# Even and odd fields on the two halves of the TensorE array, with 4-bank PSUM tiles, in a pairwise bilinear product

## Chip, cores, metric

One core of a Trainium2 chip. The metric is device time in microseconds (us) of one execution on that core. The kernel before takes 1359.69 us (median of 3 runs, 1359.48 to 1359.76). On one core a single run has no state of its own ("unknown"); where several runs were taken, all of them were fast.

## The reference

4096 rows, each with 32 fields of 64 numbers, and a 64 x 64 matrix W for each of the 496 pairs i < j of fields. All in float32; 520 MB are written.

```python
idx_i, idx_j = np.triu_indices(32, k=1)
vi = inputs[:, idx_i, :]                       # (4096, 496, 64)
vj = inputs[:, idx_j, :]
return jnp.einsum('bpd,pde->bpe', vi, W) * vj  # (4096, 496, 64)
```

## The kernel before

A row tile is 128 of the 4096 rows; there are 32. For each, TensorE multiplies x_i (turned, so that the 64 numbers of a field lie on partitions) with W for up to 16 pairs at once, into a PSUM tile. VectorE multiplies the PSUM tile with x_j into an output tile; five output tiles (groups of pairs) leave per row tile. The contraction is only 64 long: in the trace these matmuls take 64 rows of the array (`64*128`), the transposes 128 (`128*128`). The kernel uses both halves of the rows for the **same** pairs: half 0 makes the first 32 of the 64 output columns, half 1 the others.

```python
E2 = D // 2                 # 32
CH = BANK // E2             # 16 pairs a step
...
psum = ctx.enter_context(tc.tile_pool(name="psum", bufs=4, space=bass.MemoryType.PSUM))
...
def order_w(c, k, copy):    # W put in order by a copy, in pieces
    ...
    copy(rp[:r], src[:, k * EU : (k + 1) * EU])
def turn_w(c, k, rp, copy): # then turned by TensorE
    ...
# a step: m <= 16 pairs of field i
ps = psum.tile([P, 2, CH, E2], F32, tag="ps", name=f"ps_{s}")   # 2 banks, four such tiles
...
for h in range(2):
    nc.tensor.matmul(ps[:, h, ...], xT[...][h * D : (h + 1) * D, ...], wT[c][h * D : (h + 1) * D, ...], ...)
...
if i in aside and c0 == 0:            # 7 steps of 46
    nc.scalar.copy(tmp, src)
    nc.gpsimd.tensor_mul(dst, tmp, xj)
else:
    nc.vector.tensor_mul(dst, src, xj)
```

For field i to be on either half, x is turned twice, in 32 transposes of neighbouring fields (0,1), (1,2), ..., eight to a PSUM tile. W is loaded in four transfers of 128 or 112 partitions.

Of the kernel before, what the change touches and what calls it, by code (L numbers as in the profile page):

```python
# [8 lines left out]
F32 = mybir.dt.float32  # L9


@with_exitstack
def kernel(
    ctx: ExitStack,
    tc: tile.TileContext,
    x: bass.AP,
    w: bass.AP,
    out: bass.AP,
):










    nc = tc.nc  # L30

    B, F, D = x.shape
    P = 128
    NB = 2
    assert 2 * D == P and B % (NB * P) == 0
    NBLK = B // (NB * P)
    NP = F * (F - 1) // 2
    E2 = D // 2
    BANK = 512
    CH = BANK // E2  # L40
    RUN = 2 * BANK // P
    p0 = [i * (F - 1) - i * (i - 1) // 2 for i in range(F)]


    groups = [(0, 3), (3, 7), (7, 11), (11, 17), (17, F - 1)]
    cap = max(p0[b] - p0[a] for a, b in groups)

    aside = (1, 3, 5, 7, 9, 11, 13)

    cuts = [*range(0, NP, P), NP]  # L50
    wrows = list(zip(cuts[:-1], cuts[1:]))

    const = ctx.enter_context(tc.tile_pool(name="const", bufs=1))
    xpool = ctx.enter_context(tc.tile_pool(name="xpool", bufs=2))
    xtpool = ctx.enter_context(tc.tile_pool(name="xtpool", bufs=4))
    tpool = ctx.enter_context(tc.tile_pool(name="tpool", bufs=3))
    opool = ctx.enter_context(tc.tile_pool(name="opool", bufs=3))
    psum = ctx.enter_context(tc.tile_pool(name="psum", bufs=4, space=bass.MemoryType.PSUM))

    ident = const.tile([P, P], F32, tag="ident", name="ident")  # L60
    make_identity(nc, ident)

    xs = {}

    def rows_of(dram: bass.AP, blk: int) -> bass.AP:
        return dram[blk * NB * P : (blk + 1) * NB * P]

    def new_x(blk: int):

        xs[blk] = xpool.tile([P, 1 + NB * F, D], F32, tag="xs", name=f"xs_{blk}")  # L70
        nc.gpsimd.memset(xs[blk][:, 0, :], 0.0)  # L71

    def load_x(blk: int, eng, k0: int = 0, k1: int = NB):
        src = rows_of(x, blk).rearrange("(p k) f d -> p (k f) d", k=NB)
        eng.dma_start(out=xs[blk][:, 1 + k0 * F : 1 + k1 * F, :], in_=src[:, k0 * F : k1 * F, :])


    wflat = w.rearrange("p d e -> p (d e)")
    raw, wT = {}, {}
    EU = 2 * BANK // P  # L80
    NU = E2 // EU

    def load_w(c: int):

        a, b = wrows[c]
        pool, tag = ((opool, "ot"), (xpool, "xs"), (const, "w3"), (xpool, "xs"))[c]
        raw[c] = pool.tile([P, D * D], F32, tag=tag, name=f"raw_{c}")
        nc.sync.dma_start(out=raw[c][: b - a, :], in_=wflat[a:b])

    def order_w(c: int, k: int, copy):  # L90
        r = wrows[c][1] - wrows[c][0]
        rp = tpool.tile([P, EU, 2, D], F32, tag="tmp", name=f"rp_{c}_{k}")
        src = raw[c][:r, :].rearrange("p (d h e) -> p e h d", h=2, d=D)
        copy(rp[:r], src[:, k * EU : (k + 1) * EU])  # L94
        return rp

    def turn_w(c: int, k: int, rp, copy):
        r = wrows[c][1] - wrows[c][0]
        if c not in wT:
            wT[c] = const.tile([P, r, E2], F32, tag=f"w{c}", name=f"wT_{c}")  # L100
        pt = psum.tile([P, EU, P], F32, tag="ps", name=f"ptw_{c}_{k}")
        for n in range(EU):
            nc.tensor.transpose(  # L103
                pt[:, n, :r], rp[:r, n].rearrange("p h d -> p (h d)"), ident[:r, :r]
            )
        copy(wT[c][:, :, k * EU : (k + 1) * EU], pt[:, :, :r].rearrange("p e r -> p r e"))  # L106

    def turn_x(blk: int, k: int, q: int, copy):

        pt = psum.tile([P, RUN, P], F32, tag="ps", name=f"ptx_{blk}_{k}_{q}")  # L110
        for n in range(RUN):
            s = k * F + q * RUN + n
            nc.tensor.transpose(  # L113
                pt[:, n, :], xs[blk][:, s : s + 2, :].rearrange("p f d -> p (f d)"), ident
            )
        xT = xtpool.tile([P, RUN, P], F32, tag="xT", name=f"xT_{blk}_{k}_{q}")
        copy(xT, pt)  # L117
        return xT


    steps = [
        (g, i, c0, min(CH, F - 1 - i - c0))
        for g, (a, b) in enumerate(groups)
        for i in range(a, b)
        for c0 in range(0, F - 1 - i, CH)
    ]
    NS = len(steps)
    first = {}
    for s, (_, i, _, _) in enumerate(steps):
        first.setdefault(i, s)  # L130


    AHEAD = 4
    due: dict = {}
    for t in range(NBLK * NB):
        for q in range(F // RUN):
            at = t * NS + (first[q * RUN - 1] if q else 0) - AHEAD
            due.setdefault(max(0, at), []).append(("x", t // NB, t % NB, q))
    for c, at in enumerate([None, (2, 4, 5, 7), (9, 11, 13, 15), (20, 22, 25, 28)]):
        for k in range(NU) if c else ():  # L140
            due.setdefault(at[k], []).append(("w", c, k))
    LATE = 6

    new_x(0)
    load_x(0, nc.scalar, 0, 1)
    load_w(0)
    load_w(1)
    load_x(0, nc.sync, 1, NB)
    load_w(2)

    v, p, a = nc.vector.tensor_copy, nc.gpsimd.tensor_copy, nc.scalar.copy
    xT = {(0, 0, 0): turn_x(0, 0, 0, v)}
    due[0] = [d for d in due[0] if d != ("x", 0, 0, 0)]
    rps = [order_w(0, k, copy) for k, copy in ((0, v), (1, p))]
    turn_w(0, 0, rps[0], a)
    rps.append(order_w(0, 2, v))
    turn_w(0, 1, rps[1], a)
    rps.append(order_w(0, 3, v))
    turn_w(0, 2, rps[2], v)
    turn_w(0, 3, rps[3], a)  # L160

    ot = None
    for s in range(NBLK * NB * NS):
        t, st = divmod(s, NS)
        blk, kt = divmod(t, NB)
        g, i, c0, m = steps[st]
        if st == LATE and kt == 0 and blk and blk + 1 < NBLK:
            new_x(blk + 1)
            load_x(blk + 1, nc.scalar)
        for what, *args in due.get(s, ()):  # L170
            if what == "x":
                xT[tuple(args)] = turn_x(*args, a)
            else:
                c, k = args
                turn_w(c, k, order_w(c, k, (v, p)[k % 2]), a)
                if k == NU - 1 and c == 1:
                    load_w(3)
                if k == NU - 1 and c == 3:
                    new_x(1)
                    load_x(1, nc.scalar)  # L180

        base, end = p0[groups[g][0]], p0[groups[g][1]]
        pa = p0[i] + c0
        if pa == base:
            ot = opool.tile([P, cap, D], F32, tag="ot", name=f"ot_{t}_{g}")
        ps = psum.tile([P, 2, CH, E2], F32, tag="ps", name=f"ps_{s}")
        for c, (lo, hi) in enumerate(wrows):
            lo, hi = max(pa, lo), min(pa + m, hi)
            if lo < hi:
                for h in range(2):  # L190
                    n = i + 1 - h
                    nc.tensor.matmul(  # L192
                        ps[:, h, lo - pa : hi - pa, :],
                        xT[blk, kt, n // RUN][h * D : (h + 1) * D, n % RUN, :],
                        wT[c][h * D : (h + 1) * D, lo - wrows[c][0] : hi - wrows[c][0], :],
                        start=True,
                        stop=True,
                    )
        o = pa - base
        j = 1 + kt * F + i + 1 + c0  # L200
        dst = ot[:, o : o + m, :].rearrange("p m (h e) -> p m h e", h=2)
        src = ps[:, :, :m, :].rearrange("p h m e -> p m h e")
        xj = xs[blk][:, j : j + m, :].rearrange("p m (h e) -> p m h e", h=2)
        if i in aside and c0 == 0:
            tmp = tpool.tile([P, CH, 2, E2], F32, tag="tmp", name=f"tmp_{s}")
            nc.scalar.copy(tmp, src)  # L206
            nc.gpsimd.tensor_mul(dst, tmp, xj)  # L207
        else:
            nc.vector.tensor_mul(dst, src, xj)  # L209
        if pa + m == end:  # L210
            nc.sync.dma_start(  # L211
                out=rows_of(out, blk).rearrange("(p k) n d -> p k n d", k=NB)[:, kt, base:end, :],
                in_=ot[:, : end - base, :],
            )
# [27 lines left out]
```

## Time and profile before

| | before |
|---|---|
| median, us | 1359.69 |
| span of the profiled run, us | 1357.5 |
| first output issued, us | 30.0 |
| row tile 0 complete (its fifth output issued), us | 71.6 |
| last output issued, us | 1342.1 |
| so a row tile takes, us | (1342.1 - 71.6) / 31 = 40.98 |

The last four rows come from the times at which the SP queue issued the output transfers. They split any span into a **head** (to the filling of tile 0), 31 times a **pace**, and a tail; all comparisons below use this split. The profile's lines for this kernel are in the prediction: the transfers run at 401 to 433 GB/s in all but the first two and the last slice, and they are the bound.

### The profile page before, as it was taken

The numbers are of one execution on the slowest core, as the hardware profiler recorded it, in microseconds if no ns is written. First come the engines' busy times: TensorE is split into PE (matmuls) and PEld (weight loads), VectorE is DVE, ScalarE is ACT, GpSimd is POOL, SyncE is SP. The second block draws the span as 40 slices with busy tenths as digits, with TensorE's granted clock in tenths as the row PEclk, the third lists the DMA queues.
The fourth block names the chain that finished last, engine by engine and source line by source line (L and its number), as shares of the span: only waits on it lengthen the run. The fifth ranks groups of instructions, "written<-read, shape, count | busy, mean of one in ns | idle before, by whom it ended". The sixth has DMA issues, their size and how long they took to land.

```text
span 1357.5 us, 17867 instructions
## 1 busy us (share of the span) xinstructions
PE 1171.5 (86%) x7424; PEld 681.2 (50%) x7424; DVE 951.3 (70%) x1259; ACT 371.1 (27%) x367; POOL 546.2 (40%) x253
## 2 busy tenths in 40 slices
PE   5998988888888888988889888899888889888894
PEld 4554554545455454554545445455454545545552
DVE  5686876767677676766667767677776777767783
ACT  3432322222222222222322222222222322223220
POOL 4544433443333443334434334433344433444441
PEclk9998998989999999998989999999898999999997
DMA  7999999999999999999999999999999999999997
GB/s 291 388 430 431 426 424 431 431 422 426 401 424 413 430 423 412 428 409 431 410 417 425 413 433 407 421 423 410 428 412 424 426 409 424 406 431 428 417 419 335
DMA packets 26128, 562.92 MB, mean 415 GB/s; under 512 B 2896, under 2 KB 2896, under 8 KB 2896
## 3 DMA queue, kind: packets, MB, share of 16 engines
q1 hardware_dynamic: 23744, 529.28, 92.0%
q10 hardware_dynamic: 2304, 32.51, 5.7%
q8 instruction: 58, 0.95, 0.3%
q14 instruction: 22, 0.18, 0.0%
HBM read 41.68 MB, written 520.09 MB: 414 GB/s over the span
## 4 chain that ended last, share of the span: by engine, by line
DMA 50%; PE 23%; DVE 18%; POOL 4%; issue 3%; ACT 0%; DVEq 0%; SPq 0%; POOLq 0%; ACTq 0%
DMA out_dram<-ot 49%; PE ps L192 19%; DVE ot L209 18%; PE ptx L113 4%; POOL ot L207 3%; DMA raw<-in_L_rec_W_dram 1%; POOL rp L94 1%; PE ptw L103 0%; ACT tmp L206 0%; DVE rp L94 0%; DVEq L209 0%; DVE xT L117 0%; ACT wT L106 0%; SPq L211 0%; POOLq L207 0%
## 5 line engine op out<-in xcount | busy, mean ns | idle before, releaser
L209 DVE TENSOR_TENSOR ot<-ps,xs 128x1024 f32<-128x1024 f32 (+15 forms) x1248 | 938.6, 807 | 378.4 <-DMA out_dram<-ot 195.3
L192 PE MATMUL ps<-wT,xT 64*128 64x512 f32 (+14 forms) x6272 | 1025.2, 467 | 118.0 <-DVE ot L209 105.5
L192 PEld LDWEIGHTS ps<-wT,xT 64*128 64x128 f32 x6272 | 554.0, 193 | 554.6 <-DVE ot L209 281.9
L207 POOL TENSOR_TENSOR ot<-tmp,xs 128x1024 f32<-128x1024 f32 x224 | 527.3, 2360 | 623.5 <-ACT tmp L206 397.7
L206 ACT COPY tmp<-ps 128x1024 f32<-128x1024 f32 x224 | 226.7, 1012 | 465.5 <-PE ps L192 460.6
L117 ACT COPY xT<-ptx 128x1024 f32<-128x1024 f32 x127 | 128.5, 1012 | 470.2 <-PE ptx L113 470.2
L113 PE MATMUL ptx<-ident,xs 128*128 128x128 f32 x1024 | 143.8, 285 | 48.9 <-DVE ot L209 34.3
L113 PEld LDWEIGHTS ptx<-ident,xs 128*128 128x128 f32 x1024 | 113.2, 144 | 95.4 <-issue 51.3
L71 POOL MEMSET xs<- 128x64 f32 x16 | 2.4, 151 | 146.7 <-DVE ot L209 146.7
L94 POOL COPY rp<-raw 128x1024 f32<-128x1024 f32 (+1 forms) x7 | 16.1, 2299 | 16.1 <-DMA raw<-in_L_rec_W_dram 11.8
L106 ACT COPY wT<-ptw 128x1024 f32<-128x1024 f32 (+1 forms) x15 | 14.7, 984 | 28.1 <-PE ptw L103 28.1
L103 PE MATMUL ptw<-ident,rp 128*128 128x128 f32 (+1 forms) x128 | 17.0, 280 | 3.2 <-DVE rp L94 2.0
L94 DVE COPY rp<-raw 128x1024 f32<-128x1024 f32 (+1 forms) x9 | 11.0, 1233 | 12.3 <-DMA raw<-in_L_rec_W_dram 11.9
L103 PEld LDWEIGHTS ptw<-ident,rp 128*128 128x128 f32 (+1 forms) x128 | 14.1, 145 | 10.2 <-issue 5.6
L106 ACT ACT_TABLE_LOAD x1 | 1.3, 1283 | 1.2 <-PEq L229 1.2
L117 DVE COPY xT<-ptx 128x1024 f32<-128x1024 f32 x1 | 1.2, 1208 | 0.0
L106 DVE COPY wT<-ptw 128x1024 f32<-128x1024 f32 x1 | 1.2, 1208 | 0.0
masks.py:197 POOL MEMSET ident<- 128x128 f32 x1 | 0.2, 205 | 0.3 <-POOLq L229 0.3
masks.py:199 POOL TENSOR_SCALAR_AFFINE_SELECT ident<-ident 128x128 f32<-128x128 f32 x1 | 0.3, 292 | 0.0
L229 POOL MEMSET const-float32-0.0<- 128x1 f32 x1 | 0.1, 98 | 0.2 <-issue 0.2
L229 POOL MEMSET const-bfloat16-1.0<- 128x1 bf16 x1 | 0.1, 101 | 0.0
L229 POOL MEMSET const-uint8-127<- 128x1 uint8 x1 | 0.1, 101 | 0.0
(1 smaller groups left out, 0.1 us busy)
## 6 DMA issues: line engine op xcount, KB each, us to landing
out_dram<-ot SPq DMA_DIRECT2D x64, 3360.0 KB, 16.2
out_dram<-ot SPq DMA_DIRECT2D x64, 2880.0 KB, 16.7
out_dram<-ot SPq DMA_DIRECT2D x32, 3392.0 KB, 17.2
xs<-in_r_inputs_dram ACTq DMA_DIRECT2D x15, 2048.0 KB, 16.6
raw<-in_L_rec_W_dram SPq DMA_DIRECT2D x3, 2048.0 KB, 15.6
raw<-in_L_rec_W_dram SPq DMA_DIRECT2D x1, 1792.0 KB, 15.7
xs<-in_r_inputs_dram ACTq DMA_DIRECT2D x1, 1024.0 KB, 11.4
xs<-in_r_inputs_dram SPq DMA_DIRECT2D x1, 1024.0 KB, 17.7
```

Of the source, the lines that this page charges most:

```text
L71: nc.gpsimd.memset(xs[blk][:, 0, :], 0.0)
L94: copy(rp[:r], src[:, k * EU : (k + 1) * EU])
L103: nc.tensor.transpose(pt[:, n, :r], rp[:r, n].rearrange("p h d -> p (h d)"), ident[:r, :r])
L106: copy(wT[c][:, :, k * EU : (k + 1) * EU], pt[:, :, :r].rearrange("p e r -> p r e"))
L113: nc.tensor.transpose(pt[:, n, :], xs[blk][:, s : s + 2, :].rearrange("p f d -> p (f d)"), ident)
L117: copy(xT, pt)
L192: nc.tensor.matmul(ps[:, h, lo - pa : hi - pa, :], xT[blk, kt, n // RUN][h * D : (h + 1) * D, n % RUN, :], wT[c][h * D : (h + 1) * D, lo - ...
L206: nc.scalar.copy(tmp, src)
L207: nc.gpsimd.tensor_mul(dst, tmp, xj)
L209: nc.vector.tensor_mul(dst, src, xj)
L229: nc = _bacc.Bacc("TRN2", target_bir_lowering=False, num_devices=1)
```

## The change

The intent: put **different** fields on the halves, even ones on half 0 and odd ones on half 1. All 64 columns of a pair then come from one half, so a matmul has 8 pairs x 64 columns, x needs 16 transposes, not 32, and W needs no ordering before it is turned. To have fewer and longer instructions, a PSUM tile holds 2 fields x 16 pairs, 4 banks (a bank is the program's `BANK`, 512 float32 numbers a partition); four tiles of 2 banks become two of 4.

```diff
-    E2 = D // 2
-    CH = BANK // E2
+    BP = BANK // D
+    PSB = 4
+    CH = PSB // 2 * BP
...
-    psum = ctx.enter_context(tc.tile_pool(name="psum", bufs=4, space=bass.MemoryType.PSUM))
+    psum = ctx.enter_context(tc.tile_pool(name="psum", bufs=2, space=bass.MemoryType.PSUM))
...
-        nc.sync.dma_start(out=raw[c][: b - a, :], in_=wflat[a:b])
+            while a < b:
+                n = min(16, b - a)
+                c = a - row0[f]
+                dst = (raw if a < P else wT[1])[a % P : a % P + n].rearrange(
+                    "r (h d) e -> r h (d e)", h=2
+                )
...
+                    nc.sync.dma_start(out=dst, in_=src)     # 26 loads in all, of 16 rows or fewer
...
-    def order_w(c: int, k: int, copy):
...
+    def turn_w(lo: int, hi: int, e0: int, copies):
+        src = (wT[1] if c else raw)[a : a + n].rearrange("r m e -> r e m")   # strided read
...
-        ps = psum.tile([P, 2, CH, E2], F32, tag="ps", name=f"ps_{s}")
+        ps = psum.tile([P, 2, CH, D], F32, tag="ps", name=f"ps_{s}")
+        for b0 in range(0, m, BP):
+            for h in range(halves):
+                nc.tensor.matmul(
+                    ps[:, h, b0:b1, :],
+                    xT[t][h * D : (h + 1) * D, f, :],
+                    wT[r // P][h * D : (h + 1) * D, r % P : r % P + b1 - b0, :],
...
-        if i in aside and c0 == 0:
+        if (f, c0) in aside and t:                # two steps of 24
+            nc.scalar.copy(dst, src)
+            nc.gpsimd.tensor_mul(dst, dst, xj)
```

W's row for field pair f holds the matrices of an even and an odd field side by side. Field pair f has 31 - 2f rows, in steps of up to 16: 16 + 15, 16 + 13, ..., 16 + 1, then single steps.

Passages are cut from the recorded prediction, each cut marked: what it took over, without a trace that shows it, on transfers, on PSUM and on the clock; when W was to be in, with rival D that went with it; and the reason that rival C gave for a falling clock. The sum stands as it was forecast, 1360 + 8 + 31 x 0.5 = 1383, put at 1380. The cut passage on when W is in belonged to the working behind the 8 us of the head; how much of the 8 came from it is not on record. The 0.05 us for a signal is the author's estimate (the trace has 0.06 from a multiply's end to the next weight load), and so is the 0.5 us added for the mesh.

> **What bounds the kernel now.** I read the page first, then the trace in four places: what the transfer queue waited for, the chain of waits, windows of the head, and windows of stretches in which VectorE never stops. The page's rates, queues and rows:
>
> ```profile
> PE 1171.5 (86%) x7424; PEld 681.2 (50%) x7424; DVE 951.3 (70%) x1259; ACT 371.1 (27%) x367; POOL 546.2 (40%) x253
> ...
> DMA  7999999999999999999999999999999999999997
> GB/s 291 388 430 431 426 424 431 431 422 426 401 424 413 430 423 412 428 409 431 410 417 425 413 433 407 421 423 410 428 412 424 426 409 424 406 431 428 417 419 335
> ...
> q1 hardware_dynamic: 23744, 529.28, 92.0%
> q10 hardware_dynamic: 2304, 32.51, 5.7%
> ...
> L209 DVE TENSOR_TENSOR ot<-ps,xs 128x1024 f32<-128x1024 f32 (+15 forms) x1248 | 938.6, 807 | 378.4 <-DMA out_dram<-ot 195.3
> L206 ACT COPY tmp<-ps 128x1024 f32<-128x1024 f32 x224 | 226.7, 1012 | 465.5 <-PE ps L192 460.6
> L113 PE MATMUL ptx<-ident,xs 128*128 128x128 f32 x1024 | 143.8, 285 | 48.9 <-DVE ot L209 34.3
> ```
>
> The two queues take 97.7% of the span, no slice is above 433 GB/s, and VectorE's largest wait is for an output transfer to free its tile. The kernel is bound by writing 520 MB. At 430 GB/s its 562.9 MB need 1309 us; the span is 1357.5. So whatever the change does for the engines, some 48 us is all there is to win. The chain of waits gives the pace:
>
> ```profile
> 369.57 20.33 DMA out_dram<-ot
> ...
> 452.17 20.34 DMA out_dram<-ot
> ```
>
> The same wait comes back after 82.6 us, two row tiles: 41.3 us a tile. A tile moves 17.3 MB (16.25 out, half of a 2.1 MB load of x), 40.2 us at 430 GB/s. So about 1 us a tile is lost now, and the rest of the 48 us lies in the head and the tail:
>
> ```profile
> 22.00:32.00 10.00, 10.00 (x62) 5.90 (x64) 7.19 (x8) 6.02 (x6) 5.40 (x3) 1.00 0.21 88
> ```
>
> (window, length, busy time of PE, weight load, VectorE, ScalarE and GpSimd, granted clock, transfer share, GB/s.) For some 8 us the queue has nothing to write while W is ordered and turned.
>
> **Where the small figures come from.** By shape, the multiply takes 1219 ns at 1024 elements and 219 ns at 64: 1.042 ns per element plus 0.15 us. Neighbouring multiplies overlap by 0.08 us (one starts at 594.20 and lasts 1.09, the next starts at 595.21). TensorE's pace:
>
> ```profile
> 604.41 0.19 PEld L192 LDWEIGHTS ps<-wT,xT 64*128 64x128 f32 x2 [0.24 <-issue]
> 604.84 0.19 PEld L192 LDWEIGHTS ps<-wT,xT 64*128 64x128 f32 x2 [0.23 <-issue]
> 605.11 1.01 ACT L206 COPY tmp<-ps 128x1024 f32<-128x1024 f32 x1 [3.02 <-PE ps L192]
> ```
>
> A pair of 512-column matmuls, one on each half of the array, follows the last after 0.43 us, and its reader starts 0.70 us after its weight load: 0.43 plus 0.27 (I take 0.30). From a multiply's end to the next weight load it is 0.06. Eight transposes are busy 1.09 us.
>
> [...] after 123.0 to 127.0 with 0.10 us of TensorE work, the clock is 0.54 in the next 7 us.
>
> **The change part by part.**
> *Matmuls.* 196 a tile become 79; the columns stay nearly the same (W's 256 rows of 64 columns on each half against 496 of 32). Array time goes to about 14 us a tile, and 16 transposes (2.2 us) replace 32 (4.4). All off the bound.
> *VectorE.* Of 24 steps a tile 22 stay on it. Both halves of a step have equal length, so 15 surplus pairs are multiplied and overwritten: 511 x 64 = 32,704 elements, less 2 x 2048 that ScalarE and GpSimd take, 28,608. 28,608 x 1.042 = 29.8, plus 22 x 0.07 = 1.5: 31.3 us (29.3 now, 938.6/32).
> *PSUM.* Four tiles of 2 banks become two of 4. TensorE can refill a tile only while the one multiply of the other runs. A refill takes 0.06 + 0.43 + 0.43 + 0.30 = 1.22 us. After a multiply of c rows on both halves (0.15 + 0.133c) VectorE stands idle for 1.38 less that (the 0.16 are two lost overlaps): c = 9, 7, 5, 3, 1 give 0.03, 0.30, 0.56, 0.83, 1.05, together 2.8 us a tile. Each of the two steps for ScalarE (0.16 + 0.833 x 2.048 = 1.87 us) holds one of the two tiles: 1.4 and 1.1 of idle, 0.2 after: 2.7. The turn of x holds one for 2.2 + 2.0 (two copies of 1.01): 2.0 us of idle before row 3 and 1.7 before the last: 3.7. Sum 9.2.
> *Surplus pairs again.* The built program makes ten multiplies a tile wait on VectorE itself, because each overwrites a surplus pair of the one before. Some six aren't hidden behind TensorE: 6 x 0.13 (0.08 overlap, 0.05 signal) = 0.8.
> Filling a tile thus takes 31.3 + 9.2 + 0.8 = 41.3 us, against 40.2 for its transfers. Two nearly equal stages with three output tiles between them don't mesh fully; I add 0.5: 41.8, against 41.3 now.
> *Head.* No ordering, but 26 loads of W go in, [...] Walked through with the durations above: first half of W at 11.7, its 64 transposes and copies to 21.4, first multiply 22.7, first output 38 (30.0 now), then four more turns of W interleaved with steps, group 1 at 50, tile 0 filled at 78 and written at 88. Before, 19.8 MB had moved by 60 us and 28.5 were needed, so tile 0 was written at about 80: 8 us worse.
> Sum: 1360 + 8 + 31 x 0.5 = 1383; with a slightly better mesh 1370. I say **1380**.
>
> **The rivals.** (A) As above: the two-tile exchange between TensorE and VectorE paces the kernel at about the transfers' speed: 1365 to 1400. (B) Transfers stay the only bound and the 1 us a tile that is lost now comes back, since there are fewer long stops of TensorE and so fewer slow refills: 1360 + 8 - 31 x 0.7 = 1346. For it: the queue is 97.7% busy now, and before's fill, with about 30 us of VectorE a tile, has slack. Against: the change takes that slack away. (C) The clock falls [...]; pairs at 0.86 would make a tile 48 us, the kernel 1540. Against it is this stretch, in which VectorE never stops and TensorE's columns fill under 40% of the time, at full clock:
>
> ```profile
> 679.00:681.00 2.00, 2.00 (x18) 1.20 (x14) 2.00 (x4) 0.29 (x1) 0.00 (x0) 1.00 1.01 426
> 681.00:683.00 2.00, 1.85 (x14) 0.90 (x12) 2.00 (x5) 0.00 (x0) 0.00 (x0) 1.00 0.99 426
> ```
>
> [...]
>
> **Range and chances.** Each 0.3 us a tile is 9 us, and my gaps are good to about 0.8 us a tile: 1350 to 1412. Faster by 2% means under 1332.5, below what even B reaches: 0.05. Slower by 2% starts at 1386.9, just above my centre: 0.40. Within 2%: 0.55.
>
> **What would show it.** Right: VectorE's busy time up to 970 to 1010 us; its waits for TensorE up from 157 to some 250 us or more, those for output transfers down from 195; the longest waits for TensorE ahead of the two small rows at a tile's end; the transfer share below 9 in many slices; the first output at 35 us or later. Wrong: flat 425 to 430 GB/s with VectorE waiting mainly for transfers (B, and the time below 1350), or a granted clock under 0.8 (C). I'd be wrong in size if a multiply of 2048 elements took something other than 2.29 us, or if refills took much less than 1.2.

## The result

The changed kernel takes **1752.38 us** (median of 4 fast runs, 1746.95 to 1756.72), the kernel before 1359.72 in the same rounds (4 fast runs, 1359.48 to 1364.54). The ratio is 1.2875, with a 95% interval of 1.2829 to 1.2921. Ratios in this document are the mean time of one kernel's fast runs over the mean of the other's fast runs of the same rounds, so not quite the ratio of the medians. The result is exact enough to pass against the reference. The time is far outside the predicted range of 1350 to 1412.

| us | before | after | difference |
|---|---|---|---|
| first output issued | 30.0 | 95.9 | |
| tile 0 complete (head) | 71.6 | 162.6 | +91.0 |
| 31 tiles | 31 x 40.98 | 31 x 50.94 | +308.7 |
| last output issued to the end (tail) | 15.4 | 9.3 | -6.1 |
| span | 1357.5 | 1751.1 | +393.6 |

So four fifths of the loss is the steady pace, one fifth the head. The page of the kernel after; its rows of groups give busy time and mean ns of one, then idle time of that engine just before them and what ended most of it:

```profile
PE 1223.3 (70%) x5760; PEld 583.2 (33%) x5760; DVE 1061.1 (61%) x715; ACT 185.7 (11%) x134; POOL 281.5 (16%) x70
...
PEclk9678999899899999989899999989999989999997
DMA  9765787978788797777879787787877778797777
GB/s 122 97 215 248 319 382 326 391 316 335 306 339 363 326 391 319 329 309 333 368 313 395 325 339 336 329 347 335 374 338 329 322 313 355 325 392 331 300 300 327
...
q1 hardware_dynamic: 24242, 532.69, 75.1%
...
L197 PE MATMUL ps<-wT,xT 64*128 64x512 f32 (+4 forms) x5056 | 1132.4, 578 | 434.2 <-DVE ot L216 384.8
L216 DVE TENSOR_TENSOR ot<-ps,xs 128x2048 f32<-128x2048 f32 (+5 forms) x706 | 1050.4, 1512 | 584.4 <-PE ps L197 509.5
...
L117 PEld LDWEIGHTS ptw<-ident,raw 64*128 64x128 f32 x128 | 18.9, 263 | 39.2 <-issue 38.6
```

The transfers, 92% of the span's transfer time on the output queue before, fall to 75%, and most slices run at 300 to 390 GB/s. VectorE's largest wait is no longer for output transfers; it waits 509.5 us for TensorE (156.9 before). And TensorE waits 384.8 us for VectorE. Each waits for the other, and neither is busy: 70% and 61%. That is a handover with too little room, not a full engine. The waits, by who waits and for whom (us in total, times, longest us), say the same:

```profile
PEld ps L197 <- DVE ot L216: 575.8, 444, 2.4
DVE ot L216 <- PE ps L197: 509.5, 328, 3.9
...
PE ps L197 <- DVE ot L216: 384.8, 333, 2.2
```

Of the kernel before:

```profile
DVE ot L209 <- PE ps L192: 156.9, 212, 2.7
```

One handover, in the timeline of the kernel after (start us, us, engine, what, and in brackets the idle time before and what ended it):

```profile
905.67 2.29 DVE L216 TENSOR_TENSOR ot<-ps,xs 128x2048 f32<-128x2048 f32 x1 [1.42 <-issue]
...
907.88 0.55 DVE L216 TENSOR_TENSOR ot<-ps,xs 128x384 f32<-128x384 f32 x1
...
908.02 0.30 PEld L197 LDWEIGHTS ps<-wT,xT 64*128 64x128 f32 x4 [2.42 <-DVE ot L216]
...
908.55 0.19 PEld L197 LDWEIGHTS ps<-wT,xT 64*128 64x128 f32 x2 [0.23 <-issue]
908.98 0.19 PEld L197 LDWEIGHTS ps<-wT,xT 64*128 64x128 f32 x2 [0.24 <-issue]
909.41 0.19 PEld L197 LDWEIGHTS ps<-wT,xT 64*128 64x128 f32 x2 [0.24 <-issue]
...
910.05 2.29 DVE L216 TENSOR_TENSOR ot<-ps,xs 128x2048 f32<-128x2048 f32 x1 [1.63 <-PE ps L197]
```

VectorE's long multiply ends near 907.96 and frees a PSUM tile. TensorE starts to refill it at 908.02. Meanwhile VectorE has only a short tile, 0.55 us, so it stands idle for 1.63 us until 910.05. The refill took 2.03 us. The prediction had 1.22.

The refill has 4 matmuls: 2 pieces of 8 pairs for each of 2 fields, so two pairs of matmuls. But the timeline shows their weight loads in four rounds, 0.43 us apart: two at 908.02 (x4, the second loaded ahead), then one each at 908.55 and 908.98; those at 909.41 and later are loaded ahead for the next tile. From 908.02 to 910.05 four rounds of 0.43 and the signal of 0.30 fit; two rounds don't. The page agrees: 79 matmuls a tile in the program x 32 tiles are 2528, and it counts 5056. **Each float32 matmul is recorded twice** (I call each record a pass), each time with a weight load. The "x2" beside a weight load are the two halves of the array in the same pass, and a pair of 512-column matmuls takes 2 x 0.43 = 0.86 us. This could have been seen before: 196 records a tile there, where the program has 98 matmuls.

A smaller part of the pace is a clock that falls now and then. Two neighbouring row tiles (window, length, busy time of PE, weight load, VectorE, ScalarE, GpSimd with counts, granted clock, transfer share, GB/s):

```profile
313.20:366.00 52.80, 38.63 (x174) 17.80 (x174) 32.62 (x22) 5.68 (x5) 9.05 (x2) 0.87 0.83 348
366.00:415.60 49.60, 35.65 (x174) 16.56 (x174) 32.67 (x22) 5.57 (x5) 9.04 (x2) 0.97 0.77 328
```

The same 22 multiplies, equally long on VectorE, take 52.80 us at a granted clock of 0.87 and 49.60 at 0.97. A straight line through the 31 tiles gives 48.9 us plus 0.28 us for each us at half clock; a tile has 7.4 of those on average, so the clock costs some 2 us of the 50.94.

The head: loads of W at a low rate, then TensorE waiting for them. Window of the kernel after and, for comparison, of the kernel before:

```profile
20.00:30.00 10.00, 0.09 (x1) 0.12 (x2) 0.00 (x0) 0.00 (x0) 0.00 (x0) 1.00 0.96 112
```

```profile
10.00:20.00 10.00, 6.10 (x40) 5.66 (x40) 7.91 (x6) 2.94 (x3) 3.83 (x2) 1.00 0.99 424
```

(The clock's record begins with its first change, in the kernel after at 46.2 us, so the 1.00 of the first window is no reading; weight loads 0.85 us apart from 42.8 to 45.3 us, twice the 0.43 from 46.2 us on, show half clock.) The engines of the transfer queue are "busy" for 96% of the time in one and 99% in the other, but move 112 GB/s in one and 424 in the other. The busy share does not tell a slow transfer from a fast one; the GB/s do. The timeline of the kernel after has the two waits that follow:

```profile
29.91 9.50 PE L117 MATMUL ptw<-ident,raw 64*128 64x64 f32 x64 [19.63 <-DMA raw<-in_L_rec_W_dram]
...
107.93 2.41 PE L117 MATMUL ptw<-ident,wT 128*128 128x128 f32 x10 [25.61 <-DMA wT<-in_L_rec_W_dram]
```

### The profile page after: what moved, and what is told of

Same layout as the page of the kernel before. It is cut to its first block, busy times and chain, and to the rows that moved or that the text cites. A ratio compares the mean times of both kernels' runs of the same rounds, so it can differ in the third digit from the quotient of the medians.

```text
span 1751.1 us, 13667 instructions
## 1 busy us (share of the span) xinstructions
PE 1223.3 (70%) x5760; PEld 583.2 (33%) x5760; DVE 1061.1 (61%) x715; ACT 185.7 (11%) x134; POOL 281.5 (16%) x70
## 5 line engine op out<-in xcount | busy, mean ns | idle before, releaser
L197 PE MATMUL ps<-wT,xT 64*128 64x512 f32 (+4 forms) x5056 | 1132.4, 578 | 434.2 <-DVE ot L216 384.8
L216 DVE TENSOR_TENSOR ot<-ps,xs 128x2048 f32<-128x2048 f32 (+5 forms) x706 | 1050.4, 1512 | 584.4 <-PE ps L197 509.5
L197 PEld LDWEIGHTS ps<-wT,xT 64*128 64x128 f32 x5056 | 498.0, 202 | 1054.2 <-DVE ot L216 575.8
L214 POOL TENSOR_TENSOR ot<-ot,xs 128x2048 f32<-128x2048 f32 x62 | 280.6, 4526 | 1426.9 <-ACT ot L213 1426.9
L139 ACT COPY xT<-ptx 128x1024 f32<-128x1024 f32 x63 | 60.7, 1015 | 1145.4 <-PE ptx L133 1145.4
L213 ACT COPY ot<-ps 128x2048 f32<-128x2048 f32 x62 | 115.6, 1865 | 264.4 <-PE ps L197 260.3
L133 PE MATMUL ptx<-ident,xs 128*128 128x128 f32 x512 | 64.6, 281 | 18.6 <-DVE ot L216 12.0
L133 PEld LDWEIGHTS ptx<-ident,xs 128*128 128x128 f32 x512 | 56.9, 143 | 34.3 <-DVE ot L216 27.7
L117 PE MATMUL ptw<-ident,raw 64*128 64x64 f32 x128 | 19.2, 339 | 37.0 <-DMA raw<-in_L_rec_W_dram 19.6
L117 PEld LDWEIGHTS ptw<-ident,raw 64*128 64x128 f32 x128 | 18.9, 263 | 39.2 <-issue 38.6
L117 PE MATMUL ptw<-ident,wT 128*128 128x128 f32 x64 | 11.3, 338 | 28.2 <-DMA wT<-in_L_rec_W_dram 25.6
L121 ACT COPY wT<-ptw 128x1024 f32<-128x1024 f32 x8 | 8.1, 1012 | 107.9 <-PE ptw L117 75.4
```

The source lines that it names most:

```text
L117: nc.tensor.transpose(pt[:, k, :], src[:, e0 + k, :], ident[a : a + n, a : a + n])
L121: copy(wT[c][:, a : a + n, e0 + s.start : e0 + s.stop], pt[:, s, :].rearrange("p e r -> p r e"),)
L133: nc.tensor.transpose(pt[:, f, :], xs[blk % 2][:, s : s + 2, :].rearrange("p f d -> p (f d)"), ident)
L139: copy(xT[t][:, k * step : (k + 1) * step, :], pt[:, k * step : (k + 1) * step, :])
L197: nc.tensor.matmul(ps[:, h, b0:b1, :], xT[t][h * D : (h + 1) * D, f, :], wT[r // P][h * D : (h + 1) * D, r % P : r % P + b1 - b0, :], star ...
L213: nc.scalar.copy(dst, src)
```

## The experiments

What was open after reading the two traces: (1) is the 0.86 us of a pair two passes with both halves at once, or two halves one after the other? (2) Is it the number of PSUM tiles, or the new layout, that makes VectorE and TensorE wait for each other? (3) What part has the clock? (4) What makes the loads of W slow: their uneven row counts, the partitions that they write, or where they read? All single runs below have the state "unknown"; the kernel before, run in the same calls, took 1360.82 us (first call), 1359.9 (second, median of 7), 1365.21 (third, one run) and 1360.02 (fourth, median of 6).

| run | tile 0 complete | pace, us a tile | us at half clock | time, us |
|---|---|---|---|---|
| before | 71.6 | 40.98 | 110 | 1359.72 |
| after | 162.6 | 50.94 | 302 | 1752.38 |
| same_half (wrong result) | 192.2 | 118.47 | 3688 | 3875.89 |
| two_bank | 154.8 | 40.76 | 138 | 1433.77 |
| balanced | 153.5 | 43.28 | 59 | 1507.64 |
| before_two | 86.9 | 55.04 | 238 | 1805.51 |
| busy_pe | 155.0 | 48.52 | 58 | 1670.15 |
| w_rows128 (wrong result) | 106.1 | 50.86 | 248 | 1694.29 |
| w_two_queues | 146.0 | 51.08 | 325 | 1740.41 |
| w_dst_near (wrong result) | 135.3 | 50.73 | 264 | 1718.78 |
| w_dst_far (wrong result) | 116.8 | 50.72 | 271 | 1700.03 |
| w_src_far (wrong result) | 162.2 | 50.89 | 326 | 1751.04 |
| two_bank_q | 137.5 | 40.76 | 169 | 1419.57 |
| two_bank_far | 115.6 | 40.76 | 107 | 1394.36 |

The granted clock of TensorE is 1.00 or 0.50 in every record of these runs; the column counts the time at 0.50 within the span, from the first change of the clock on.

Not every expectation held. A little faster than the expected range were two_bank, balanced and busy_pe (by 6, 2 and 5 us); before_two was 16 us slower than it. Clearly missed were the rate of w_dst_far (206 GB/s, 350 or more expected), tile 0 of w_rows128 (106.1 us, 75 to 95 expected) and of w_two_queues (146.0, 115 to 140), and two_bank_q (1419.57 us, 1375 to 1410).

### same_half: both fields on one half of the array

The result is wrong on purpose: both matmuls of a pair read partitions 0 to 63.

```diff
-                    xT[t][h * D : (h + 1) * D, f, :],
-                    wT[r // P][h * D : (h + 1) * D, r % P : r % P + b1 - b0, :],
+                    xT[t][0:D, f, :],
+                    wT[r // P][0:D, r % P : r % P + b1 - b0, :],
```

> Both matmuls of a pair read the lower 64 rows of the array (wrong result on purpose; as many instructions of the same shapes). Theory 1, the two halves never ran at the same time and a 512-column fp32 matmul takes 0.43 us by itself: nothing changes, 1720 to 1780 us, about 51 us a row tile. Rival, the halves overlap and 0.86 us is what the pair takes together: putting both on one half doubles array time to about 57 us a tile, a tile takes 66 us or more, the kernel 2200 us or more.

3875.89 us, 118.47 a tile. A window and part of the weight loads' timeline:

```profile
900.00:1000.00 100.00, 95.90 (x138) 42.37 (x137) 26.20 (x17) 5.66 (x4) 8.99 (x2) 0.52 0.31 134
```

```profile
917.80 0.34 PEld L197 LDWEIGHTS ps<-wT,xT 64*128 64x128 f32 x1 [0.52 <-issue]
918.66 0.33 PEld L197 LDWEIGHTS ps<-wT,xT 64*128 64x128 f32 x1 [0.52 <-issue]
```

Weight loads now come one at a time, 0.86 us apart: single passes, at half clock (0.52). Four of them make a pair, 3.4 us against 0.86. In one of the few stretches at full clock (1377.0 to 1380.4 us) single passes are 0.43 us apart:

```profile
1379.28 0.19 PEld L197 LDWEIGHTS ps<-wT,xT 64*128 64x128 f32 x1 [0.24 <-issue]
1379.71 0.19 PEld L197 LDWEIGHTS ps<-wT,xT 64*128 64x128 f32 x1 [0.24 <-issue]
```

So of this factor of four, two is the clock. The other two is what the halves were saving, so in the kernel after **the halves do run at once**, and the theory that they never overlap falls. The 0.86 is two passes. What nobody expected is the clock: 0.52 for nearly the whole run, although TensorE is 95.9% busy. After 200 us it is full in only 23 stretches of 3.4 us (x is turned 30 times in that time), each beginning within 5 us of the start of the 16 transposes that turn x, the only instructions left that use 128 rows of the array. The trace of w_rows128, below, has the same: while W is turned on 64 rows, TensorE never stops and the clock is half,

```profile
18.30:27.70 9.40, 9.40 (x64) 9.25 (x64) 1.23 (x1) 1.01 (x1) 0.00 (x0) 0.50 1.01 432
```

it becomes full at 33.9 us, 3.8 us after pairs on both halves begin, and is half again at 40.7 us, after 4.4 us of 64-row work without a pause. So in these traces being busy is not enough; busy on 64 rows goes with half clock. No run was made to test this alone.

### two_bank: the new layout with four PSUM tiles

```diff
-    PSB = 4
+    PSB = 2
...
-    psum = ctx.enter_context(tc.tile_pool(name="psum", bufs=2, space=bass.MemoryType.PSUM))
+    psum = ctx.enter_context(tc.tile_pool(name="psum", bufs=4, space=bass.MemoryType.PSUM))
```

Steps become 2 fields x 8 pairs; x and W are turned in pieces of 2 banks. Field layout, loads of W and turning in place stay.

> Four PSUM tiles of 2 banks (2 fields x 8 pairs) in place of two of 4, all else as in the changed kernel, the load of W too. Theory: the steady pace is set by two tiles that are exchanged between TensorE and VectorE; with four, TensorE works ahead, VectorE's wait for it falls from 510 us to under 150, and a row tile falls from 50.9 us to the transfers' 40.5 to 42; the first tile stays at about 160 us; kernel 1440 to 1490 us. Rival, TensorE or VectorE is simply too slow in the new layout: 1650 us or more.

1433.77 us, correct; the pace is 40.76. The page:

```profile
DMA  9865999999999999999999999999999999999998
GB/s 132 93 121 237 401 421 433 421 433 425 426 417 427 422 420 418 422 434 421 419 422 422 417 416 432 422 420 422 424 421 418 429 412 431 420 422 419 422 416 375
...
L218 DVE TENSOR_TENSOR ot<-ps,xs 128x1024 f32<-128x1024 f32 (+3 forms) x1218 | 1145.5, 992 | 161.7 <-DMA out_dram<-ot 74.3
```

VectorE waits for output transfers again, as before the change, and though it is busy for 1145.5 us, 95 more than after, the kernel is 319 us shorter. Its wait for TensorE is 50.6 us in all (under 150 expected). The whole loss in pace comes back, with a remainder of 0.22 us a tile in the layout's favour. The loss left, 74 us, is nearly all head.

### before_two: the old layout with two PSUM tiles

The converse: the kernel before, with one figure changed.

```diff
-    psum = ctx.enter_context(tc.tile_pool(name="psum", bufs=4, space=bass.MemoryType.PSUM))
+    psum = ctx.enter_context(tc.tile_pool(name="psum", bufs=2, space=bass.MemoryType.PSUM))
```

> The kernel before, with two PSUM tiles of 2 banks in place of four, nothing else changed. Theory: it is the number of PSUM tiles, not the new layout, that takes TensorE's lead away; with a pair of 512 columns at 0.86 us and the multiply at 1.22, my step-by-step sum gives 52 us a row tile (40.98 now), kernel 1690 to 1790 us. Rival, the two-tile exchange hurts only the new layout with its uneven steps: under 1450 us.

1805.51 us, correct, 55.04 a tile. The page's row, to be held against the 378.4 us of idle time before it in the kernel before:

```profile
L209 DVE TENSOR_TENSOR ot<-ps,xs 128x1024 f32<-128x1024 f32 (+15 forms) x1248 | 979.3, 812 | 788.0 <-PE ps L192 693.7
```

Without any of the change's other parts, two tiles in place of four cost 14 us a tile. Together with two_bank: **the number of PSUM tiles is what costs the pace in both layouts** (in two_bank their size changes with it), and fields on the halves cost nothing in it.

### balanced: equal steps

If the long refill hides behind a short multiply, the uneven cuts (16 + 7, 16 + 5, 16 + 3, 16 + 1) are what makes two tiles so bad.

```diff
+    def even(r):
+        k = -(-r // CH)
+        q = CH if r == 23 else -(-r // k)
+        return [(c0, min(q, r - c0)) for c0 in range(0, r, q)]
...
-        for c0 in range(0, rows[f], CH)
+        for c0, m in even(rows[f])
```

> Still two tiles of 4 banks, but a field's rows are cut evenly (19 as 10 and 9, not 16 and 3; 23 stays 16 and 7). Theory: the idle time comes from a long refill that has only a short multiply of the other tile to hide behind; even cuts bring a row tile from 50.9 to 43 to 46 us, the kernel to 1510 to 1610 us with the same number of instructions of VectorE. Rival, two tiles as such or the surplus pairs cost it: within 30 us of 1752.

1507.64 us, correct; 43.28 a tile. The page:

```profile
L221 DVE TENSOR_TENSOR ot<-ps,xs 128x1920 f32<-128x1920 f32 (+8 forms) x706 | 1056.6, 1523 | 331.6 <-PE ps L202 303.4
```

The same 706 multiplies with nearly the same total work (1056.6 us, 1050.4 after), and 7.7 us a tile less: VectorE's wait for TensorE falls from 509.5 to 303.4. The time at half clock falls too, from 302 to 59 us, so this run alone does not separate the two; the next one does, and leaves about 48.52 - 43.28 = 5.2 us a tile to the even cuts.

### busy_pe: no pauses for the clock to fall in

The short steps' matmuls are made 2 to 7 times over (the same values are written again), so that TensorE is busy while VectorE is.

```diff
-            for h in range(halves):
+            again = {7: 2, 5: 3, 3: 5, 1: 7}.get(m, 1) if c0 else 1
+            for h in [*range(halves)] * again:
```

> The changed kernel with the matmuls of its short steps (7, 5, 3, 1 rows) repeated 2, 3, 5, 7 times into the same place: TensorE works while it would only wait, the result stays right. In the changed kernel's trace a row tile takes 48.9 us plus 0.28 us for each us at half clock (7.3 us a tile on average). Theory: the clock falls because TensorE idles; kept busy it stays up, a tile takes 48.5 to 49.5 us, the kernel 1675 to 1715 us in spite of more matmuls. Rival, the clock follows something else or doesn't matter: 1740 us or more.

1670.15 us, correct. The steady stretch of this kernel, and of the kernel after:

```profile
155.00:1659.00 1504.00, 1189.08 (x6990) 610.59 (x6990) 1011.31 (x682) 173.51 (x123) 280.63 (x62) 1.00 0.84 355
```

```profile
162.50:1741.80 1579.30, 1144.99 (x5378) 529.63 (x5378) 1013.21 (x683) 173.56 (x123) 280.58 (x62) 0.93 0.80 338
```

More work on TensorE makes the kernel 82 us faster: the clock is 1.00, not 0.93, and a tile takes 48.52 us, close to the 48.9 that the straight line over the tiles of the kernel after gives for full clock. So the clock has 2.4 of the 9.96 us lost per tile, and the exchange at full clock the rest.

### The head: w_rows128, w_two_queues, w_dst_near, w_dst_far, w_src_far

w_rows128 loads the same bytes in 4 transfers of 128 rows (so wrong rows of W, and a wrong result on purpose).

```diff
-                    nc.sync.dma_start(out=dst, in_=src)      # 26 loads in all, of 16 rows or fewer
...
+            nc.sync.dma_start(
+                out=dst.rearrange("r (h d) e -> r h (d e)", h=2)[:, h, :],
+                in_=wflat[lo // P * 2 * P // 2 + h * P : lo // P * 2 * P // 2 + h * P + P],
+            )
```

> W comes in by four loads of 128 rows (2 MB each, wrong rows on purpose), the rest as in the changed kernel. Theory: the 16-row loads [...] run at 110 GB/s, and they hold the start back; with 128 rows the load runs at 400 GB/s, tile 0 is filled by 75 to 95 us and not by 162, and the kernel takes 1660 to 1685 us, at the same 51 us a row tile. Rival, the turning of W holds it back: tile 0 later than 130 us, 1720 us or more.

1694.29 us; tile 0 is complete at 106.1, not 162.6. In the window the rate is 429 GB/s:

```profile
20.00:30.00 10.00, 7.74 (x54) 7.55 (x53) 2.41 (x2) 2.02 (x2) 0.00 (x0) 0.50 1.01 429
```

w_two_queues keeps the 26 loads and issues them in turn from SP and GpSimd.

```diff
+                    turn[0] ^= 1
-                    nc.sync.dma_start(out=dst, in_=src)
+                    (nc.sync if turn[0] else nc.gpsimd).dma_start(out=dst, in_=src)
```

> The changed kernel with the loads of W alternating between SP's queue and GpSimd's (result right). [...] W comes in at some 200 GB/s and not 110, tile 0 is filled at 115 to 140 us and not 162, the kernel takes 1700 to 1735 us. Rival, the source or the number of descriptors limits it: 1745 us or more.

1740.41 us, correct; tile 0 at 146.0. The rate stays near where it was, so the expectation that two queues run side by side at twice the rate failed:

```profile
20.00:30.00 10.00, 0.00 (x0) 0.00 (x0) 0.00 (x0) 0.00 (x0) 0.57 (x1) 0.50 1.04 118
```

From 20 to 80 us no 10 us have more than 126 GB/s. There are fewer dips (111 to 126 GB/s from 40 to 70 us, against 77 to 110 in the kernel after), and W is in at 91.2 us, not 107.9; which of the loads gain was not looked into. So the loads' shape sets the rate, and a second queue hardly lifts it (118 GB/s against 112 from 20 to 30 us). Three runs of one call separate where the rows go from where they come from. w_dst_near has 16 equal loads of 16 rows into 16 neighbouring partitions; w_dst_far writes every eighth partition instead; both read the same, wrong rows. w_src_far is the kernel after with a source whose rows lie 31 matrices apart.

```diff
+            rows16 = slice(16 * q, 16 * q + 16)        # w_dst_near
+            rows16 = slice(q, P - 7 + q, 8)            # w_dst_far
...
-                        ap=[src.ap[0], (rows[f] * D * D, 2), (1, D * D)],
+                        ap=[(31 * D * D, 16), (15 * D * D, 2), (1, D * D)],   # w_src_far
```

The figures before each rival stand for the theory that the partitions written set the rate. What was said of the reason is cut, as it is in w_rows128, w_two_queues and two_bank_far, since no run shows it.

> The changed kernel with W in sixteen equal loads of 16 rows into 16 neighbouring partitions (wrong rows on purpose), so no uneven counts. The two queues did not help, so the cause of the slow load (110 GB/s against 430 with 128 rows) is open. [...] still about 110 GB/s. Rival, uneven row counts (13, 7, 5 ...) [...]: this one then runs at 350 GB/s or more and tile 0 is filled by 110 us.

> The same sixteen loads, same source addresses, but the rows of one load go to every 8th partition. [...] 350 GB/s or more, tile 0 filled by 105 to 115 us, kernel 1690 to 1710 us. Rival, the source (16 rows of 16 KB close together in memory) limits it: 110 GB/s as with neighbouring partitions, 1745 us or more.

> The loads of the changed kernel (neighbouring partitions, uneven counts), with the source rows of one load 31 rows apart (wrong rows on purpose). [...] still about 110 GB/s, 1740 us or more. Rival, the source limits it: 300 GB/s or more, about 1700 us.

Windows of w_dst_near, of w_dst_far and of w_src_far, in this order:

```profile
30.00:35.00 5.00, 4.46 (x31) 4.27 (x30) 1.22 (x1) 1.38 (x2) 0.00 (x0) 1.00 0.93 108
```

```profile
30.00:35.00 5.00, 5.00 (x37) 5.00 (x36) 1.23 (x1) 1.01 (x1) 0.00 (x0) 0.50 1.02 206
```

```profile
20.00:30.00 10.00, 0.15 (x1) 0.18 (x2) 0.00 (x0) 0.00 (x0) 0.00 (x0) 0.50 0.95 112
```

The distance in the source does nothing (tile 0 at 162.2, against 162.6). Equal loads of 16 rows, with all else the same, have 108 GB/s into neighbouring partitions and 206 into every eighth one. With all 128 partitions in a load (w_rows128) it was 429, with more rows in a load, too. So the partitions written set the rate between 108 and 206; the step from there to 429 changes the rows of a load as well. Why neighbouring partitions take longer, no run shows.

In the head's 91.0 us, read off as a ladder of completion times of tile 0: 162.6 to 135.3 (27.3 us) for equal, fuller and fewer loads; to 116.8 (18.5) for the partitions; to 106.1 (10.7) for transfers of all 128. The first rung changes both the number of loads (26 to 16) and their row counts, and no run separates these two.

The rest, 106.1 to 71.6, is 34.5 us that no loading explains, and no run divides it. Three things are in the traces. Turning W: a weight load of a strided row takes 263 ns, of an ordered one 145, and TensorE is busy for 30.5 us with turning (19.2 and 11.3), against 17.0. The two PSUM tiles, which row tile 0 uses as well: before_two has it complete at 86.9 us, 15.3 later than before, with nothing else changed. The clock: half for 37.6 of the first 106.1 us in w_rows128, while before's record, from 14.9 us on, has no half clock in its head. What each has of the 34.5 was not tested.

### two_bank_q and two_bank_far: the best of the parts together

two_bank_q is two_bank plus the two queues. two_bank_far is two_bank with the loads cut so that each writes every eighth partition; the order is put right by the copy out of PSUM, and W's first 128 rows are all loaded and turned before the first step:

```diff
-                n = min(16, b - a)
+                n = min(16 - a % 16, b - a)
+                q = a % P // 16 + 8 * (a % 16)
-                dst = (raw if a < P else wT[1])[a % P : a % P + n].rearrange(
+                dst = (raw if a < P else wT[1])[q : q + 8 * n - 7 : 8].rearrange(
...
-                wT[c][:, a : a + n, e0 + s.start : e0 + s.stop],
-                pt[:, s, :].rearrange("p e r -> p r e"),
+                wT[c].rearrange("p (q i) e -> p q i e", i=16)[:, :, :, e0 + s.start : e0 + s.stop],
+                pt[:, s, :].rearrange("p e (i q) -> p q i e", q=8),
```

> Four tiles of 2 banks and W over two queues together: row tiles at 40.8 us as with two_bank, tile 0 at 100 to 130 us and not 155: 1375 to 1410 us, still behind the kernel before (1360), whose first tile is filled at 72 us.

> Four tiles of 2 banks, and each load of W puts its rows on every 8th partition (the copies out of PSUM put the columns back in order, so the result is right). The cuts at 16 rows and at fields give 29 loads of uneven size. W should come in at about 200 GB/s, tile 0 be filled at 100 to 125 us (154.8 in two_bank, 71.6 before), row tiles take 40.8 us: 1380 to 1410 us. [...] No theory has it faster than the kernel before.

Both are correct. two_bank_q: 1419.57 us (4 fast runs, 1416.31 to 1421.56), ratio to before 1.0431 (1.0403 to 1.0460). two_bank_far: 1394.36 us (4 fast runs, 1393.20 to 1395.22), ratio 1.0244 (1.0219 to 1.0270). Neither beats the kernel before. In two_bank_far the pace is 40.76 against 40.98, a gain of 7 us over 31 tiles, and the head is 115.6 against 71.6, a loss of 44. (Its loads of uneven size ran at 164 GB/s from 20 to 30 us, under the 206 of equal ones.) So, as far as these runs show, the new layout would be worth some 7 us if W came in and was turned as fast as before.

## Why the prediction was wrong, point by point

**The bound before: right.** The transfers were the bound; two_bank, which brings them back to 416 to 434 GB/s in most slices, runs at nearly the old pace.

**The mechanism: right.** Rival A, the two-tile exchange between TensorE and VectorE, is what paces the kernel after. VectorE's waits for TensorE rose ("to some 250 us or more", measured 509.5), and those for output transfers are no longer in the list of waits. One sign failed: the longest waits were to stand ahead of the two small rows at a tile's end. They average 1.6 and 0.5 us there, but 3.8 us ahead of a tile's first multiply and 2.0 to 2.6 us ahead of the long multiplies that follow 5 rows, 3 rows or 1. The multiply of 2048 elements was put at 2.29 us, and its row by shape has it:

```profile
L216 DVE TENSOR_TENSOR ot<-ps,xs 128x2048 f32<-128x2048 f32 x194 | 444.6, 2292 | 245.4 <-PE ps L197 184.4 <-issue 61.0
```

ScalarE's copy (1.87 us predicted, 1865 ns on the page) was right as well. VectorE's total was foretold as 970 to 1010 us; it is 1061, 1050 of it multiplies.

**The step that failed** is this sentence: "A pair of 512-column matmuls, one on each half of the array, follows the last after 0.43 us". What follows after 0.43 us is the second pass of the same pair. The lines quoted for it were right, their reading was not: "x2" was taken for the whole of a pair. The check was at hand, for the prediction writes "196 a tile become 79" and so compares records (two to a matmul) with matmuls.

The consequences follow the prediction's own working. A refill is 0.06 + 0.86 + 0.86 + 0.30 = 2.08 us, not 1.22 (measured 2.03). Put into the same sums, the gaps after short multiplies come to some 8.2 us, not 2.8 (those after 15, 13 and 11 rows now count too), and each of ScalarE's two steps costs 0.86 more. So VectorE's gaps grow from 9.2 to some 16 us a tile, and a tile takes 48.0 to 48.5 us, not 41.8. From the two windows under busy_pe, VectorE's idle time is (1579.30 - 1013.21) / 31 = 18.3 us a tile in the kernel after and (1504.00 - 1011.31) / 31 = 15.9 in busy_pe, where the clock is held up and a tile takes 48.52. The array's time a tile was also halved by the same slip, "about 14 us".

**Rival C: dismissed on the same slip.** It had "pairs at 0.86 would make a tile 48 us", as the consequence of a falling clock, and was set aside since "TensorE's columns fill under 40% of the time, at full clock". With pairs at 0.86 they fill twice that. So the number 48 was right for another reason than the one given, and the clock came on top: 302 us at half clock, which costs 2.4 us a tile by busy_pe. C's own sign, a mean clock under 0.8, did not come: it was 0.91.

**The head: right direction, far too small.** The prediction said 8 us; it is 91. When W was to be in is cut from it; that working started from the full rate. The rate was in fact a quarter of the 429 GB/s that loads of 128 rows have: 112 GB/s, the partitions written being one measured part of it (108 against 206 GB/s). The last piece of W landed at 107.9 us. The sign "first output at 35 us or later" was met by 95.9. The ladder above puts 45.8 us on load counts and partitions, 10.7 more on not using all 128 at once, and leaves 34.5 undivided between turning W, the two tiles and the clock.

**Rival B: falsified** in the kernel after. two_bank shows what it had in mind, but with 0.22 us a tile gained where it foretold 0.7.

**Rival D**, the uneven load of W alone, is cut from the prediction, since no trace shows what it rested on. Equal and fewer loads (w_dst_near) gained 27.3 us of the head, but with equal loads the rate was still 108 GB/s: unevenness or the number of loads was a part, and the partitions, which no rival named, another.

**The range** allowed for gaps "good to about 0.8 us a tile", that is for errors in adding durations up. These sums do add up (the pace of before was taken as 41.3 us from one pair of waits; over all tiles it is 40.98). It allowed nothing for a duration read wrongly, and that one was 8 us a tile.

## What to carry to other kernels

Before a duration goes into a sum, count the records per instruction of the program: half the rate hides easily in an "x2" (5056 records for 2528 matmuls here). When a PSUM tile is doubled and their number halved, look whether the refill still runs ahead (two tiles in place of four took a row tile from 40.98 to 55.04 us in before_two); ask what VectorE does while the one free tile is filled, above all when a long step follows a short one. And look at which partitions a load writes before its size: 16 rows a load came at 108 GB/s into neighbouring partitions and at 206 into every eighth, and loads of 128 rows at 429.
